# PSUM as one tile of eight banks, and row maxima and exponentials of two heads by one instruction each

## The chip, the core and the metric

The kernel runs on one core of a Trainium2 chip. The metric is device time in microseconds (us) of one execution. A core has TensorE (PE; its weight loads are listed as PEld), VectorE (DVE), ScalarE (ACT), GpSimd (POOL) and SyncE (SP, which here issues DMAs). Each engine works through its own instructions in program order and waits on semaphores for the others. PSUM, the memory that matmuls write, has eight banks of 512 fp32 values on each of 128 partitions.

## What is computed

The reference is a stack of four layers on x of shape 8 x 512 x 128 (batch, sequence, width). Each half layer is `x = x + layernorm(f(layernorm(x)))`.

```
x = x + ln(L0_attn(ln(x)));  x = x + ln(L0_ffn(ln(x)))     # softmax attention; RWKV channel mix
x = x + ln(L1_attn(ln(x)));  x = x + ln(L1_ffn(ln(x)))     # test-time training; switch experts
x = x + ln(L2_attn(ln(x)));  x = x + ln(L2_ffn(ln(x)))     # linear attention; expert-choice experts
x = x + ln(L3_attn(ln(x)));  x = x + ln(L3_ffn(ln(x)))     # softmax attention with rope; staggered experts
```

The change concerns the two softmax attentions, L0 and L3. Both have 16 heads of width 8:

```
scores = q @ k.T  (512 x 512 per batch and head, L3 divides by sqrt(8))
out    = softmax(scores, axis=-1) @ v
```

## The kernel before

The work is one program with no loops on the chip; Python loops write out every instruction, and the order in which they are written is the order on each engine. Four parts follow each other: L0 attention with the L0 feed-forward, the L1 learner and routing in its background; a middle part (rest of L1, all of L2); L3 attention with the L3 feed-forward in its background; and a short tail that ends the last feed-forward.

Both attentions use `Attention.run` (L380). A *call* n is one batch with four heads; there are 32 calls in each attention. A call is cut into NJ = 4 blocks of 128 rows, and a *step* g handles one block, so an attention has 128 steps, plus lead and end. A tile `qk` holds q and k of the four heads, each head on its own group of 32 partitions, so that matmuls of four heads occupy four row groups of TensorE. An fp32 matmul shows as two MATMUL records and two weight loads in the trace.

The softmax is made in two passes over the scores:

- `score(g, h)` (L387) makes the scores with queries on the partitions (matmul at L393 into a bank called `at_s`), and VectorE takes the negated row maximum (L394) into `at_mx`.
- `maxima(n, mx)` (L368) transposes the maxima of a whole call on TensorE (L372), copies them (L374) and sends them by four DMAs (L376) into a spare row of `qk`, so that the second product subtracts them.
- `weigh(g, h)` (L396) makes the scores again, transposed (matmul at L400 into a bank called `at_st`), and ScalarE takes the exponential (L403) into `at_e`.
- `total_up(n)` (L405) multiplies the exponentials of a call with v (L411, 32 MATMUL records in one bank, `at_o`) and copies the result (L419). `finish(n)` (L421) transposes it (L425) and divides by the sum that a column of ones gave (L428, L429).

`score` runs LEAD = 7 steps ahead of `weigh`. At each end of an attention, seven steps therefore have only one of the two. In a full step the order of the four score heads and the four exponential heads is s0, t2, s1, t3, then background work that costs little (`bg.between`), then s2, t0, s3, t1:

```
for i in (0, 2):
    for h in range(2):
        if is_s: score(ahead, i + h)
        if is_t: weigh(g, 2 - i + h)
    if i == 0 and (is_s or is_t): bg.between()
```

After that come, where they are due, `maxima`, `total_up` and `finish`, and then `bg.pull` (L296), which writes out pieces of background work. `Background` (L253) is a planner: every piece yields its estimated cost on TensorE and VectorE, and `pull` takes pieces until 5.0 us of TensorE or 3.0 us of VectorE (L0), or 3.3 and 2.5 us (L3), are used. In L3 these pieces are the projection of the next batch (L1766 and the VectorE and GpSimd work after it) and the feed-forward of finished batches (`hidden`, L1923 and L1924; `result`, L1930 and L1933). The costs do not depend on how long anything takes on the chip, so the order of the background is fixed by the program.

Every PSUM user takes a bank by `cx.bank(name)` (L118), which turns through RING = 8 tags:

```
self.turn[0] += 1
return self.ps.tile([P, 512], F32, name=name, tag=f"bank{self.turn[0] % self.RING}", bufs=1)
```

A tag has one buffer, so the ninth bank asked for waits until all users of the first have finished with it. Eight heads of a full step take eight banks; then the background's banks follow in the same ring.

Of the kernel before, what the change touches and what calls it, by code (L numbers as in the profile page):

```python
# [9 lines left out]
F32 = mybir.dt.float32  # L10
I32 = mybir.dt.int32
AF = mybir.ActivationFunctionType
ALU = mybir.AluOpType
AX = mybir.AxisListType
PSUM = bass.MemoryType.PSUM
DRAM = bass.MemoryType.DRAM

P = 128
# [3 lines left out]
NJ = S // P  # L22
# [48 lines left out]
class Ctx:  # L71


    def __init__(self, es: ExitStack, tc: tile.TileContext, consts: bass.AP):
        self.tc = tc
        nc = self.nc = tc.nc
        pool = lambda name, bufs, **kw: es.enter_context(tc.tile_pool(name=name, bufs=bufs, **kw))
        self.keep = pool("keep", 1)
        self.shared = pool("shared", 2)
        self.dram = pool("dram", 1, space=DRAM)  # L80

        self.c = self.keep.tile([P, C_ALL], F32, name="consts_sb", tag="consts_sb")
        nc.sync.dma_start(self.c, consts)
        self.ident = self.c[:, C_ID : C_ID + P]
        self.triu = self.c[:, C_TRIU : C_TRIU + P]
        self.ones = self.keep.tile([P, P], F32, name="ones", tag="ones")
        nc.vector.memset(self.ones, 1.0)
        self.mhalf = self.keep.tile([P, 8], F32, name="mhalf", tag="mhalf")
        nc.vector.memset(self.mhalf, -0.5)
        self.x = [self.keep.tile([P, NJ, D], F32, name=f"x{b}", tag=f"x{b}") for b in range(B)]  # L90

        self.home = self.keep

        self.ps = pool("ps", 1, space=PSUM)
        self.turn = [0]
        es.enter_context(tc.manual_schedule())

        self.brisk = False
# [17 lines left out]
            yield other  # L116

    def bank(self, name):  # L118
        self.turn[0] += 1
        return self.ps.tile([P, 512], F32, name=name, tag=f"bank{self.turn[0] % self.RING}", bufs=1)  # L120

    def work(self, shape, name, bufs=2, dtype=F32):
        return self.w.tile(shape, dtype, name=name, tag=name, bufs=bufs)
# [197 lines left out]
class Attention:  # L321
# [58 lines left out]
    def run(self, n_calls, load, dst, done, scale, bg):  # L380


        cx, nc = self.cx, self.cx.nc
        total = NJ * n_calls
        mx, es, ots = {}, {}, {}

        def score(g, h):  # L387
            n, c = divmod(g, NJ)
            qk = self.qks[n % self.NQK][32 * h : 32 * h + 32]
            if n not in mx:  # L390
                mx[n] = cx.work([P, NJ, 4], "at_mx", bufs=3)
            s = cx.bank("at_s")
            nc.tensor.matmul(s, qk[:, 0, c * P : (c + 1) * P], qk[:, 1, :], start=True, stop=True)  # L393
            nc.vector.tensor_reduce(mx[n][:, c, h : h + 1], s, AX.X, ALU.max, negate=True)  # L394

        def weigh(g, h):  # L396
            n, c = divmod(g, NJ)
            qk = self.qks[n % self.NQK][32 * h : 32 * h + 32]
            s = cx.bank("at_st")
            nc.tensor.matmul(s, qk[:, 1, c * P : (c + 1) * P], qk[:, 0, :], start=True, stop=True)  # L400
            if g not in es:
                es[g] = cx.work([P, 4, S], "at_e", bufs=5)
            nc.scalar.activation(es[g][:, h, :], s, AF.Exp, scale=scale)  # L403

        def total_up(n):  # L405
            o = cx.bank("at_o")
            vp = self.pads[n % self.NPAD]
            for c in range(NJ):
                e = es.pop(NJ * n + c)
                for h in range(4):  # L410
                    nc.tensor.matmul(  # L411
                        o[32 * h : 32 * h + 32, :],
                        vp[:, c, h, :],
                        e[:, h, :],
                        start=(c == 0),
                        stop=(c == NJ - 1),
                    )
            ots[n] = cx.work([P, S], "at_ot")
            nc.scalar.copy(ots[n], o)  # L419

        def finish(n):  # L421
            ot = ots.pop(n)
            t = cx.bank("at_ops")
            for c in range(NJ):
                nc.tensor.transpose(t[:, c * P : (c + 1) * P], ot[:, c * P : (c + 1) * P], cx.ident)  # L425
            t = t.rearrange("p (c h d) -> p c h d", c=NJ, h=4)
            rec = cx.work([P, NJ, 4, 1], "at_rec")
            nc.vector.reciprocal(rec, t[:, :, :, 8:9])  # L428
            nc.vector.tensor_mul(dst(n), t[:, :, :, 0:8], rec.to_broadcast([P, NJ, 4, 8]))  # L429
            done(n)  # L430

        for g in range(-self.LEAD - self.LOAD, total + 2):
            ahead = g + self.LEAD
            is_s, is_t = 0 <= ahead < total, 0 <= g < total
            n, c = divmod(ahead + self.LOAD, NJ)
            if c == 0 and 0 <= n < n_calls:
                self.fill(n, *load(n))
            for i in (0, 2):

                for h in range(2):  # L440
                    if is_s:
                        score(ahead, i + h)
                    if is_t:
                        weigh(g, 2 - i + h)
                if i == 0 and (is_s or is_t):
                    bg.between()
            spent = 0.0
            n, c = divmod(ahead - 4, NJ)
            if c == 0 and 0 <= n < n_calls:
                self.maxima(n, mx.pop(n))  # L450
            n, c = divmod(g - NJ, NJ)
            if c == 0 and 0 <= n < n_calls:
                total_up(n)
                spent += 3.6
            if c == 1 and 0 <= n < n_calls:
                finish(n)
                spent += 0.5
            if is_s or is_t:
                bg.pull(spent)
# [147 lines left out]
class Mix:  # L607
# [16 lines left out]
    def load(self):  # L624
        cx, nc = self.cx, self.cx.nc
        W_r, W_k, W_v, mu_r, mu_k = self.args
        self.mu = cx.const([D, 2], "mu")
        nc.sync.dma_start(self.mu[:, 0:1], mu_r.rearrange("(d o) -> d o", o=1))
        nc.sync.dma_start(self.mu[:, 1:2], mu_k.rearrange("(d o) -> d o", o=1))
        raws = []  # L630
        for i, w in enumerate((W_r, W_k, W_v)):
            raws.append(cx.work([P, D], f"l0f_raw{i}", bufs=1))
            nc.sync.dma_start(raws[-1], w)
        self.nu = cx.const([D, 2], "nu")
        yield
        yield
        yield
        nc.vector.tensor_scalar(self.nu, self.mu, -1.0, 1.0, ALU.mult, ALU.add)
        t = cx.bank("l0f_w_ps")
        for i in range(3):  # L640
            nc.tensor.transpose(t[:, i * P : (i + 1) * P], raws[i], cx.ident)
        w = cx.const([P, 3, P], "w0f")
        nc.scalar.copy(w[:, 0:2, :].rearrange("p i d -> p (i d)"), t[:, : 2 * P])

        nc.scalar.mul(w[:, 2, :], t[:, 2 * P : 3 * P], 0.5)
        self.wr, self.wk, self.wv = (w[:, i, :] for i in range(3))
        yield 0.4
# [1414 lines left out]
```

## Time and profile before

| | us |
|---|---|
| median of 3 runs | 2136.73 |
| lowest and highest run | 2125.67, 2138.96 |
| the profiled execution | 2132.52 |
| its span, first to last instruction | 2130.7 |
| PE busy in the span | 1772.0 |
| DVE busy | 1290.8 |
| ACT busy | 1085.9 |
| first and last score matmul, L0 attention (L393) | 40.6, 708.7 |
| first and last score matmul, L3 attention (L393) | 1339.4, 2018.2 |

The profile is one execution of the program. An engine's busy time is the union of its instructions' durations. "PE" counts matmuls, which overlap; their ends are modelled by the profiler's reader. A group line gives line, engine, operation, output <- inputs, shapes and count, then the busy time in us and the mean duration in ns, then the idle time of the engine just before these instructions and what ended it. A line of waits names who waited for whom, total us, times, and the longest. In the order of time, a line gives start, length, engine, line and operation; instructions of one kind that follow each other are merged (x2, x8).

### The profile page before, as it was taken

To read this page: it belongs to the slowest core of one execution; us is meant where nothing else is said; L and a number is where in the kernel's file an instruction comes from. 1 tells how busy PE (TensorE), PEld (TensorE's weight loads), DVE (VectorE), ACT (ScalarE), POOL (GpSimd) and SP (SyncE) were. 2 spreads that over 40 slices of the span, in tenths; PEclk is the share of its full clock that TensorE was granted. 3 is DMA by queue.
4 is the path that set the end of the run, shared out by engine and by line. 5 is a ranking of instruction groups with operands and counts; after the bars stand their busy time and mean duration, and the time that the engine had idled before them with its cause. 6 is when DMAs were issued, how large, how long until landed. Compare 5 with 4: busy or idle time off the path is not lost.

```text
span 2130.7 us, 31833 instructions
## 1 busy us (share of the span) xinstructions
PE 1772.0 (83%) x10886; PEld 1012.4 (48%) x10886; DVE 1290.8 (61%) x4012; ACT 1085.9 (51%) x2272; POOL 500.2 (23%) x566
## 2 busy tenths in 40 slices
PE   3999999898989967649446773799999999999996
PEld 1444545454534456437335552444554454545454
DVE  2777786777777665546447422777666666665522
ACT  1566655555554732346552221366666565665653
POOL 1001111112121122442523485222212121110001
PEclk7999988899988887659565786799999999999998
DMA  5212101011100032016214132111101010100000
GB/s 127 39 33 39 34 16 38 14 39 22 32 16 15 14 104 83 23 27 180 79 50 124 24 42 36 31 32 29 27 9 31 11 27 12 29 12 6 9 6 10
DMA packets 198064, 81.83 MB, mean 38 GB/s; under 512 B 97604, under 2 KB 189674, under 8 KB 197904
## 3 DMA queue, kind: packets, MB, share of 16 engines
q1 hardware_dynamic: 190224, 73.61, 14.3%
q0 software_dynamic: 7680, 6.19, 1.9%
q8 instruction: 87, 1.43, 0.3%
q14 instruction: 73, 0.60, 0.1%
HBM read 45.25 MB, written 31.59 MB: 36 GB/s over the span
## 4 chain that ended last, share of the span: by engine, by line
PE 55%; DVE 23%; ACT 6%; issue 6%; POOL 5%; DMA 3%; SPq 2%; POOLq 0%; ACTq 0%; DVEq 0%
PE at_o L411 11%; PE at_s L393 11%; DVE at_mx L394 8%; PE at_st L400 6%; PE l3f_y_ps L1930 5%; PE l3f_h_ps L1923 5%; DVE ln_st L203 2%; PE flip L239 2%; POOL l2f_out L1686 2%; POOL ln_rs L194 1%; PE l1f_h_ps L1155 1%; PE l1f_y_ps L1177 1%; POOL l2f_xg L1081 1%; PE at_ops L425 1%; DVE ln_mv L205 1%
## 5 line engine op out<-in xcount | busy, mean ns | idle before, releaser
L394 DVE TENSOR_REDUCE at_mx<-at_s 128x1 f32<-128x512 f32 x1024 | 642.3, 681 | 302.3 <-PE at_st L400 233.9
L393 PE MATMUL at_s<-qk 32*128 32x512 f32 x2048 | 612.0, 655 | 35.6 <-DMA qk<-qk_zero 21.3
L403 ACT ACTIVATE at_e<-at_st 128x512 f32<-128x512 f32 x1024 | 535.7, 597 | 193.6 <-PE at_st L400 152.4
L400 PE MATMUL at_st<-qk 32*128 32x512 f32 x2048 | 610.2, 655 | 18.4 <-DVE at_mx L394 12.6
L194 POOL TENSOR_TENSOR ln_rs<-ln_ve,mhalf 128x4 f32<-128x4 f32 x136 | 138.3, 1017 | 837.5 <-DVE ln_ve L188 773.7
L393 PEld LDWEIGHTS at_s<-qk 32*128 32x128 f32 x2048 | 232.2, 194 | 177.4 <-issue 57.7
L400 PEld LDWEIGHTS at_st<-qk 32*128 32x128 f32 x2048 | 240.5, 192 | 111.7 <-issue 41.8
L411 PE MATMUL at_o<-at_e,pad_v 128*32 128x512 f32 x2048 | 254.2, 641 | 14.8 <-DVE at_mx L394 14.8
L411 PEld LDWEIGHTS at_o<-at_e,pad_v 128*32 128x32 f32 x2048 | 66.9, 117 | 197.5 <-issue 173.8
L1930 PEld LDWEIGHTS l3f_y_ps<-w3f,l3f_hT 128*128 128x128 f32 x1024 | 131.8, 197 | 46.3 <-issue 26.8
L1930 PE MATMUL l3f_y_ps<-w3f,l3f_hT 128*128 128x128 f32 x1024 | 136.9, 282 | 3.2 <-ACT l3f_hT L1924 2.0
L419 ACT COPY at_ot<-at_o 128x512 f32<-128x512 f32 x64 | 37.5, 585 | 199.5 <-PE at_o L411 199.5
L1923 PE MATMUL l3f_h_ps<-l3f_xT,w3f 128*128 128x512 f32 x256 | 131.2, 611 | 0.0
L1924 ACT ACTIVATE l3f_hT<-l3f_h_ps,w3f_b1c 128x512 f32<-128x512 f32 x128 | 85.0, 683 | 64.1 <-PE l3f_h_ps L1923 64.0
L1933 DVE SCALAR_TENSOR_TENSOR l3f_o<-l3f_y_ps,l3f_w,l3f_o 128x128 f32<-128x128 f32 x128 | 44.4, 348 | 93.3 <-PE l3f_y_ps L1930 93.1
L217 ACT ACTIVATE l_xn<-x,ln_off,ln_rs 128x128 f32<-128x128 f32 x96 | 39.5, 482 | 81.5 <-DVE ln_off L211 75.4
L239 PE MATMUL flip<-consts_sb,l_xn 128*128 128x128 f32 x96 | 29.6, 398 | 54.4 <-ACT l_xn L217 54.1
L203 DVE BATCH_NORM_STATS2 ln_st<-x 128x6 f32<-128x128 f32 x256 | 55.2, 278 | 18.2 <-POOL x L937 12.4
L1686 POOL DMA_INDIRECT l2f_out<-l2f_y,l2f_idx x32 | 50.5, 1579 | 21.9 <-DVE l2f_y L1683 13.1
L1923 PEld LDWEIGHTS l3f_h_ps<-l3f_xT,w3f 128*128 128x128 f32 x256 | 42.2, 194 | 23.9 <-issue 10.0
L1773 POOL TENSOR_TENSOR l_qk<-l_r,consts_sb 128x256 f32<-128x256 f32 x32 | 21.9, 686 | 133.2 <-DVE l_r L1768 133.2
L366 POOL COPY pad_v<-l_in 128x128 f32<-128x128 f32 x32 | 9.4, 294 | 185.4 <-DMA l_in<-l_v 147.9
(412 smaller groups left out, 2551.0 us busy)
## 6 DMA issues: line engine op xcount, KB each, us to landing
l1f_w<-in_L_ffn_w SPq DMA_DIRECT2D x32, 256.0 KB
l2f_parts<-l2f_out SPq DMA_DIRECT2D x32, 256.0 KB
l2f_out<-l1f_zero SPq DMA_DIRECT2D x24, 256.0 KB
l_qk<-l_qkT SPq DMA_DIRECT2D x16, 256.0 KB
qk<-l_qk SPq DMA_DIRECT2D x128, 32.0 KB
qk<-at_mt SPq DMA_DIRECT2D x256, 2.0 KB
qk<-l_qkT SPq DMA_DIRECT2D x128, 32.0 KB
l2f_x<-l2f_rows SPq DMA_DIRECT2D x8, 272.0 KB
```

The lines of the kernel that those rows point to most:

```text
L194: self.nc.gpsimd.tensor_tensor(rs, ve, self.mhalf[:, :NJ], ALU.pow)
L203: nc.vector.bn_stats(st[:, j, :], src[:, j, :])
L239: self.nc.tensor.transpose(t[:, j * P : (j + 1) * P], src[:, j, :], self.ident)
L393: nc.tensor.matmul(s, qk[:, 0, c * P : (c + 1) * P], qk[:, 1, :], start=True, stop=True)
L394: nc.vector.tensor_reduce(mx[n][:, c, h : h + 1], s, AX.X, ALU.max, negate=True)
L400: nc.tensor.matmul(s, qk[:, 1, c * P : (c + 1) * P], qk[:, 0, :], start=True, stop=True)
L403: nc.scalar.activation(es[g][:, h, :], s, AF.Exp, scale=scale)
L411: nc.tensor.matmul(o[32 * h : 32 * h + 32, :], vp[:, c, h, :], e[:, h, :], start=(c == 0), stop=(c == NJ - 1),)
L1686: nc.gpsimd.indirect_dma_start(out=self.pairs.summed[s], out_offset=bass.IndirectOffsetOnAxis(ap=idx[e][:, s : s + 1], axis=0), in_=ys[e][ ...
L1923: nc.tensor.matmul(hp, self.w1[:, e, f * P : (f + 1) * P], xt, start=True, stop=True)
L1924: nc.scalar.activation(hts[e][:, f], hp, AF.Relu, bias=self.b1c[:, f, e : e + 1])
L1930: nc.tensor.matmul(yp[:, :D], hts[e][:, f, js], self.w2[:, e, f, :], start=(f == 0), stop=(f == NF - 1))
```

## The change

PSUM becomes one tile of eight banks, allocated once. `bank` returns a slice of one bank, and the new `twin` returns a slice of two neighbouring banks, starting at an even one; if the turn is odd, one bank is passed over. Waits between users of a bank now come from overlapping accesses to that tile, instead of from giving back a buffer.

`score` and `weigh` each handle two heads. Their matmuls move to `products`, which writes two heads into the two halves of a twin. One reduction then reads both banks (128 x 2 x 512) and writes two maxima per row, and one exponential reads both banks and writes two heads of `at_e`. In each half step, the two products for the exponentials are written first, then the two for the maxima, then the exponential, then the reduction. So the order of heads on TensorE is t2, t3, s0, s1, and after `bg.between` t0, t1, s2, s3. In a full step the banks go, in ring order, to a pair t, a pair s, a pair t and a pair s.

```
-        self.ps = pool("ps", 1, space=PSUM)
+        self.banks = pool("ps", 1, space=PSUM).tile([P, self.RING, 512], F32, name="banks", tag="banks")
...
     def bank(self, name):
+        k = self.turn[0]
         self.turn[0] += 1
-        return self.ps.tile([P, 512], F32, name=name, tag=f"bank{self.turn[0] % self.RING}", bufs=1)
+        return self.banks[:, k % self.RING, :]
+
+    def twin(self, name):
+
+        k = self.turn[0] + self.turn[0] % 2
+        self.turn[0] = k + 2
+        return self.banks[:, k % self.RING : k % self.RING + 2, :]
...
-        def score(g, h):
+        def products(s, g, i, side):
+
             n, c = divmod(g, NJ)
-            qk = self.qks[n % self.NQK][32 * h : 32 * h + 32]
+            for h in (i, i + 1):
+                qk = self.qks[n % self.NQK][32 * h : 32 * h + 32]
+                nc.tensor.matmul(
+                    s[:, h - i, :],
+                    qk[:, side, c * P : (c + 1) * P],
+                    qk[:, 1 - side, :],
+                    start=True,
+                    stop=True,
+                )
+
+        def score(g, i, s):
+            n, c = divmod(g, NJ)
             if n not in mx:
                 mx[n] = cx.work([P, NJ, 4], "at_mx", bufs=3)
-            s = cx.bank("at_s")
-            nc.tensor.matmul(s, qk[:, 0, c * P : (c + 1) * P], qk[:, 1, :], start=True, stop=True)
-            nc.vector.tensor_reduce(mx[n][:, c, h : h + 1], s, AX.X, ALU.max, negate=True)
-
-        def weigh(g, h):
-            n, c = divmod(g, NJ)
-            qk = self.qks[n % self.NQK][32 * h : 32 * h + 32]
-            s = cx.bank("at_st")
-            nc.tensor.matmul(s, qk[:, 1, c * P : (c + 1) * P], qk[:, 0, :], start=True, stop=True)
+            nc.vector.tensor_reduce(mx[n][:, c, i : i + 2], s, AX.X, ALU.max, negate=True)
+
+        def weigh(g, i, s):
             if g not in es:
                 es[g] = cx.work([P, 4, S], "at_e", bufs=5)
-            nc.scalar.activation(es[g][:, h, :], s, AF.Exp, scale=scale)
+            nc.scalar.activation(es[g][:, i : i + 2, :], s, AF.Exp, scale=scale)
...
-                for h in range(2):
-                    if is_s:
-                        score(ahead, i + h)
-                    if is_t:
-                        weigh(g, 2 - i + h)
+                if is_t:
+                    st = cx.twin("at_st")
+                    products(st, g, 2 - i, 1)
+                if is_s:
+                    s = cx.twin("at_s")
+                    products(s, ahead, i, 0)
+                if is_t:
+                    weigh(g, 2 - i, st)
+                if is_s:
+                    score(ahead, i, s)
```

## The prediction

> **What bounds the kernel now.** I read the page's totals first, then busy time by stage, then the chain of the work that ended last by stage, then the waits of TensorE's weight loads, and last one step of the loop in order of time. The stages in the second view are the first attention (45 to 735 us), the middle (735 to 1340), the last attention (1340 to 2052) and the tail.
>
> ```profile
> span 2130.7 us, 31833 instructions
> ...
> PE 1772.0 (83%) x10886; PEld 1012.4 (48%) x10886; DVE 1290.8 (61%) x4012; ACT 1085.9 (51%) x2272; POOL 500.2 (23%) x566
> ...
> PE 55%; DVE 23%; ACT 6%; issue 6%; POOL 5%; DMA 3%; SPq 2%; POOLq 0%; ACTq 0%; DVEq 0%
> ```
> ```profile
> 45.00:735.00 690.00, 634.17 (x4040) 311.86 (x4037) 509.95 (x1427) 398.17 (x845) 104.36 (x128) 0.91 0.14 28
> 735.00:1340.00 605.00, 387.39 (x1875) 298.38 (x1877) 292.45 (x1299) 224.01 (x501) 245.55 (x243) 0.71 0.27 69
> 1340.00:2052.00 712.00, 677.55 (x4590) 352.19 (x4587) 465.57 (x1188) 431.96 (x871) 132.92 (x162) 0.98 0.09 20
> ```
>
> The columns after the stage's length are PE, PEld, DVE, ACT and POOL busy, then TensorE's granted clock. In the last attention PE is busy 677.55 of 712 us (95%), VectorE only 465.57 (65%), ScalarE 431.96 (61%). In the first attention PE is busy 634.17 of 690 (92%), VectorE 509.95 (74%), ScalarE 398.17 (58%). So neither of the two engines whose instructions are merged is full. The chain by stage agrees: in the last attention PE has 74% of it and VectorE 19%; in the first, 59% and 29%, with "DVE at_mx L394" alone at 13.5% and 11.6%. The middle has no attention and the change leaves it alone.
>
> How do the reductions come onto the chain when VectorE is a third idle? Through the ring of banks. The weight loads' waits in the last attention (us in total, times, longest) say who waits:
>
> ```profile
> PEld at_mx_ps L372 <- DVE at_mx L394: 29.0, 31, 2.1
> ...
> PEld at_o L411 <- DVE at_mx L394: 19.3, 23, 1.7
> ...
> PEld l3f_y_ps L1930 <- DVE at_mx L394: 12.9, 26, 1.2
> ...
> PEld l_qkv_ps L1766 <- DVE at_mx L394: 10.3, 13, 1.2
> ```
>
> None of these reads anything that the latest reductions wrote (`maxima`, L370, wants reductions of an earlier step). They want a bank. A step with both kinds of scores takes eight banks, the whole ring, so the first background matmul after it gets the bank of the step's first score, and must wait for that score's reduction. One such step:
>
> ```profile
> 1503.84 1.29 DVE L394 TENSOR_REDUCE at_mx<-at_s 128x1 f32<-128x512 f32 x2 [0.34 <-PE at_st L400]
> 1503.94 1.08 ACT L403 ACTIVATE at_e<-at_st 128x512 f32<-128x512 f32 x2 [1.36 <-PE at_st L400]
> 1504.07 0.59 PE L400 MATMUL at_st<-qk 32*128 32x512 f32 x1
> 1504.08 0.60 PE L393 MATMUL at_s<-qk 32*128 32x512 f32 x2
> 1504.09 0.59 PE L400 MATMUL at_st<-qk 32*128 32x512 f32 x1
> 1504.61 0.16 PEld L411 LDWEIGHTS at_o<-at_e,pad_v 128*32 128x32 f32 x8 [0.76 <-DVE at_mx L394]
> ```
>
> The reader is to see a coincidence. Rounds of four matmuls on four row groups follow each other every 0.43 us (1503.22, 1503.65, 1504.08), so the last round has streamed by 1504.51. The first reduction ends at 1503.84 + 0.68 = 1504.52, and L411 starts 0.09 us later. Streaming and the bank's release end together: nothing is lost, and there is no slack either.
>
> **The change, part by part.** (1) *Merged reductions.* 1024 reductions become 512 of two rows of 512.
>
> ```profile
> L394 DVE TENSOR_REDUCE at_mx<-at_s 128x1 f32<-128x512 f32 x1024 | 642.3, 681 | 302.3 <-PE at_st L400 233.9 <-PE at_s L393 67.2
> L1322 DVE TENSOR_REDUCE l2a_n<-l2a_sq 128x32 f32<-128x256 f32 x32 | 11.2, 412 | 12.2 <-ACT l2a_sq L1317 12.2
> ```
>
> From 256 to 512 elements the duration grows by 681 - 412 = 269 ns, 1.05 ns per element, and L1322 has 32 rows in one instruction, so rows cost nothing visible. A merged one takes 681 + 512 x 1.05 = 1.22 us. Two back to back now take 0.60 (start to start, median of neighbours in the trace) + 0.68 = 1.28. Saved: 0.06 per pair, 512 x 0.06 = 32 us of VectorE. The Trainium skill, "Perfetto Trace Analysis", section "Optimizing Scalar/DVE Operations", puts the per-instruction access overhead of VectorE on PSUM at about 125 ns, which would make it an estimated 512 x 0.125 = 64 us; the row says half, because start to start already shows most of the fixed part hidden. I take the row. The same section says that grouping improves throughput "if the engine is saturated", and that if these engines are not saturated but cause bubbles on other engines, "breaking up instructions may allow work to be completed sooner". That is the rule against this change: at 65 to 74% busy its condition for grouping is not met, and the reductions' bubbles on PE are the waits above. With 125 ns the gain of (5) would be 176 x 0.125/1.28 = 17 us and the sum +27; by the second half, nothing is gained where PE waits, and (3) is the price.
>
> (2) *Merged exponentials.* Two now take 0.48 + 0.60 = 1.08 us (1503.94 above).
>
> ```profile
> L403 ACT ACTIVATE at_e<-at_st 128x512 f32<-128x512 f32 x1024 | 535.7, 597 | 193.6 <-PE at_st L400 152.4 <-PE at_s L393 39.2
> L1338 ACT ACTIVATE l2a_qkv<-l2a_qkv 128x1024 f32<-128x1024 f32 x8 | 8.3, 1041 | 0.0
> ```
>
> L643 (256 elements, 372 ns) and L419 (512, 585 ns) give 0.83 ns per element, so 597 + 426 = 1.02 us; the nearest row of that length is 1.04. I take 1.02: 0.06 per pair, 31 us of ScalarE, off the chain (ScalarE has 4% of it in both stages).
>
> (3) *The bank's release.* This is the part that decides. The twin for exponentials is now taken first, so the first background matmul after a full step gets a bank of the first exponential pair and waits for the whole merged instruction: 1503.94 + 1.02 + 0.08 (release to start, as at 1504.52 to 1504.61) = 1505.04 instead of 1504.61, 0.43 later. I looked at all 121 such steps of each stage in the trace and replaced the start of the first background matmul by the later of "streaming over + 0.09" and "first exponential's start + 1.10". Last attention: 113 steps have background work; in 66 it started both right after the first reduction and within 0.16 us of the end of streaming, and it moves by +0.43 each (28.4 us); 9 others move by 1.5 us in all; in 13 the reduction was late because VectorE was on other work, and it moves forward, -3.0 us. Together +26.9. PE idles only 34 us of 712 here, so most of it passes to the end; its share lies between PE's part of the chain, 0.74, and 1. I take 0.85: **+23 us**. First attention: 36 + 9 steps move by +32.7 us, 18 with a late reduction by -16.4. With PE at 59% of the chain the first counts +19; of the second I count half, -8, since where VectorE is late the third bank or the next twin waits for it anyway. **+11 us**.
>
> (4) *The turn between PE and VectorE.* Score matmuls that wait for a reduction's bank: 76 weight loads in the first attention, 29 in the last ("PEld at_s L393 <- DVE at_mx L394: 35.7, 76, 2.6" and "12.1, 29, 1.5"). Today the first head restarts while the second is still reduced. With twins both banks come free together at the end of the pair (0.06 sooner than the second), both products are made, and then 1.22 us is reduced where 0.68 was left: 1.22 - 0.68 - 0.06 = 0.48 longer per turn. At VectorE's chain shares: 76 x 0.48 x 0.29 + 29 x 0.48 x 0.19 = **+13 us**. Bounds: 0 (these waits lie beside others) and 105 x 0.48 = 50.
>
> (5) *Shorter reductions on the chain.* 13.5% of 690 plus 11.6% of 712 is 176 us; times 0.06/1.28 gives **-8 us**. The lead and end of each stage, seven steps with only one kind of score, are bound by that engine: 28 pairs x 0.06 for reductions and the same for exponentials, **-3 us**.
>
> (6) *At nothing.* The matmuls are the same, still four row groups in turn, each head in a bank of its own; the rounds overlap as now unless the two pairs are released apart (a rival). The bank skipped to even out a twin costs a slot in steps with an odd number of background banks; the next score's release by the background reader is as now. Single-bank users elsewhere keep their order. Pairs are already ready together: in 97% of cases the second reduction of a pair starts within 0.65 us of the first, so waiting for both products costs nothing. No DMA or SP or POOL work moves; `maxima` (L374 to L376) issues its four DMAs behind the same L372, up to 0.43 later, four steps before anyone needs them. Behind the waiting matmul on PE stands all the rest of the step; late next are the background's readers and then the next step's scores.
>
> Sum: 23 + 11 + 13 - 8 - 3 = +36 us. The profiled execution took 2132.52 (span 2130.7 and 1.8 around it), so 2168.5; the median of the runs is 4.2 above it, so **2173 us** is forecast.
>
> **Rivals.** *Absorbed* (0.27): the new wait stands where PE would have waited a little later anyway, and (3) and (4) pass on by 40% of what I take: 19 - 11 = +8, 2145 us. For it: 45% of the first attention's chain is not PE. Against it: PE at 95% in the last. *Faster* (0.13): exponentials go first and are no longer held up by a late reduction, so the score rounds are split less. Counting first starts within 0.2 us, the first attention has 716 rounds where 512 would do. A round is 0.43 us of PE, 0.25 at PE's share of the chain. The break-even is 36/0.25 = 144 of the 204 excess rounds; if all go and the -16.4 of late steps counts in full: 36 - 51 - 8 = -23, 2113 us. Against it: many splits come from waits that remain. *More splits* (0.10): pairs released apart turn a round of four into two of two, also in the last attention, where 412 of 618 rounds have all four. If 70 of its 256 half steps split, 70 x 0.86 x 0.85 = +51 on top, 2224 us. *One tile, one wait* (0.03): if the waits were kept for the whole tile and not by bank, PE would stand still during reductions, 256 steps x some 2.4 us = 2750 us; this would be the change not doing what it says.
>
> **How the numbers follow.** The likeliest case has 0.47, with 2150 to 2198 as its own range ((3) at PE's share or in full, (4) at 0 or double). Leaving out the whole-tile case, half of "more splits" and two thirds of "faster" (0.17 in all) gives 2118 to 2215. One per cent, about what a measurement of this kernel can tell from no change, is 21 us: slower by more than that needs over 2158. Likeliest beyond that line 0.44, with more splits and one tile 0.57; within it 0.30; faster 0.13.
>
> **What the profile after would show.** Merged reductions at about 1220 ns and exponentials at 1020. The first background loads after a step (L372, L411, L1766, L1923, L1930) waiting for the exponential instead of the reduction, 0.4 us longer in the last attention, where the stage should grow by some 20 us. "Single" rounds gone. The middle as long as before. I would be wrong if the last attention is not longer, if weight loads still name the reduction first, or if rounds of four are clearly more frequent in the first attention.

## The result, and the profile after

| | before | after |
|---|---|---|
| median of runs on the same chip, us | 2136.03 | 2165.2 (2161.47 to 2168.76) |
| ratio, 95% interval | 1 | 1.0145 [1.0107, 1.0183] |
| profiled execution, us | 2132.52 | 2164.64 |
| L0 attention and the middle, us | 1297.8 | 1306.4 |
| L3 attention, us | 712.5 | 736.1 |
| rounds of score matmuls in L0; in L3 | 716; 618 | 629; 595 |

The kernel became 1.45% slower, some 31 us. The forecast was 2173 us. A stage here runs from its first score matmul to the first of the next stage, and the L3 attention ends with its last exponential. Before the change its first score matmul is at 1338.4 us; the 1339.4 in the table of the kernel before is 1.0 too late. L0 and the middle are taken together, because the border between them moves by some microseconds from one profile to the next. Of the 32.1 us by which the two profiled executions differ, the L3 attention has 23.6 and all that lies ahead of it 8.6.

The page of the changed kernel, totals and the two merged groups (busy time, mean ns of one, idle time before them and what ended it):

```profile
span 2162.7 us, 31192 instructions
...
PE 1744.0 (81%) x10886; PEld 976.6 (45%) x10886; DVE 1259.5 (58%) x3500; ACT 1060.4 (49%) x1760; POOL 501.2 (23%) x566
...
L411 DVE TENSOR_REDUCE at_mx<-banks 128x2 f32<-128x1024 f32 x512 | 611.4, 1218 | 354.0 <-PE banks L399 351.5
...
L416 ACT ACTIVATE at_e<-banks 128x1024 f32<-128x1024 f32 x512 | 504.7, 1019 | 227.2 <-PE banks L399 217.1
```

VectorE does 31.3 us less and ScalarE 25.5 us less, and the end comes later. The reader is to see that the saving and the loss are on different engines. Busy time by stage of the changed kernel (length, PE, PEld, DVE, ACT, POOL, then the granted clock) shows where PE stands still:

```profile
45.00:744.70 699.70, 613.45 (x4100) 294.60 (x4096) 499.51 (x1196) 391.50 (x606) 106.15 (x130) 0.91 0.14 28
744.70:1346.90 602.20, 382.18 (x1811) 294.34 (x1811) 287.81 (x1275) 215.82 (x484) 244.62 (x240) 0.70 0.27 69
1346.90:2083.00 736.10, 673.59 (x4584) 337.33 (x4585) 448.94 (x931) 420.65 (x615) 133.00 (x162) 0.98 0.09 19
```

The last attention of the kernel before, by the same bounds:

```profile
1338.40:2050.90 712.50, 678.05 (x4586) 352.91 (x4586) 465.23 (x1187) 431.37 (x871) 132.92 (x162) 0.97 0.09 20
```

In the last attention PE is busy for 673.59 us, 4.5 less than before (678.05 in the same stage), but idle for 62.5 instead of 34.5. The clock is the same within 0.01 (0.97 before), so it is idle time and not slower matmuls. The waits of TensorE's weight loads in this stage say for whom:

```profile
PEld banks L379 <- ACT at_e L416: 32.4, 29, 2.1
PEld banks L424 <- ACT at_e L416: 27.1, 26, 1.5
PEld banks L1941 <- ACT at_e L416: 19.9, 18, 1.5
...
PEld banks L1784 <- ACT at_e L416: 14.4, 13, 1.5
...
PEld banks L1948 <- ACT at_e L416: 6.8, 6, 1.1
```

These are the transposed maxima (L379), the product with v (L424), `hidden` (L1941), the projection (L1784) and `result` (L1948). The prediction showed four of them under their old line numbers (L372, L411, L1766, L1930); the fifth, `hidden`, stood lower in the list of before:

```profile
PEld l3f_h_ps L1923 <- DVE at_mx L394: 7.3, 13, 0.8
```

Before, the five waited 78.8 us in total for the reduction "at_mx"; now it is 100.6 us for the exponential "at_e". One such step of the changed kernel, in order of time:

```profile
1515.95 1.04 PE L399 MATMUL banks<-qk 32*128 32x512 f32 x8
1516.23 1.94 ACT L416 ACTIVATE at_e<-banks 128x1024 f32<-128x1024 f32 x2 [1.33 <-PE banks L399]
1516.23 2.36 DVE L411 TENSOR_REDUCE at_mx<-banks 128x2 f32<-128x1024 f32 x2 [0.78 <-PE banks L399]
...
1517.30 0.59 PE L1784 MATMUL banks<-w3a,xnT 128*128 128x384 f32 x1 [0.31 <-ACT at_e L416]
```

The first merged exponential runs from 1516.23 for 1.02 us, to 1517.25; the projection's matmul, which reads nothing of it, starts at 1517.30, when it has let go of its two banks. The last matmul's modelled end is 1516.99, so even by that cautious end PE lost 0.31 us. Over the full steps of the stage that have background work, the median time from the end of streaming (start of the step's last score matmul plus 0.43) to the first background matmul, called the gap here, is 0.459 us after, 0.088 before; the sum of these gaps is 59.5 and 29.8 us.

### The profile page after: what moved, and what is told of

Its sections match the earlier page's. It is cut to its first block, busy times and chain, and to the rows that moved or that the text cites. A ratio compares the mean times of both kernels' runs of the same rounds, so it can differ in the third digit from the quotient of the medians.

```text
span 2162.7 us, 31192 instructions
## 1 busy us (share of the span) xinstructions
PE 1744.0 (81%) x10886; PEld 976.6 (45%) x10886; DVE 1259.5 (58%) x3500; ACT 1060.4 (49%) x1760; POOL 501.2 (23%) x566
## 4 chain that ended last, share of the span: by engine, by line
PE 30%; DVE 9%; ACT 8%; issue 5%; POOL 4%; DMA 2%; SPq 0%; POOLq 0%; ACTq 0%; DVEq 0%
PE banks L399 7%; PE banks L424 5%; PE banks L1948 5%; PE banks L1941 4%; ACT at_e L416 4%; DVE at_mx L411 3%; PE banks L246 2%; POOL l2f_out L1704 2%; DVE ln_st L210 1%; POOL ln_rs L201 1%; POOL l2f_xg L1099 1%; PE banks L1784 1%; PE banks L1489 1%; ACT ln_out L224 1%; DMA l_o<-l1f_given,l1f_place 1%
## 5 line engine op out<-in xcount | busy, mean ns | idle before, releaser
L411 DVE TENSOR_REDUCE at_mx<-banks 128x2 f32<-128x1024 f32 x512 | 611.4, 1218 | 354.0 <-PE banks L399 351.5
L399 PE MATMUL banks<-qk 32*128 32x512 f32 x4096 | 632.8, 667 | 70.0 <-ACT at_e L416 26.8
L416 ACT ACTIVATE at_e<-banks 128x1024 f32<-128x1024 f32 x512 | 504.7, 1019 | 227.2 <-PE banks L399 217.1
L399 PEld LDWEIGHTS banks<-qk 32*128 32x128 f32 x4096 | 254.9, 197 | 310.0 <-issue 117.6
L201 POOL TENSOR_TENSOR ln_rs<-ln_ve,mhalf 128x4 f32<-128x4 f32 x136 | 138.5, 1019 | 864.3 <-DVE ln_ve L195 801.3
L424 PE MATMUL banks<-at_e,pad_v 128*32 128x512 f32 x2048 | 239.8, 609 | 10.9 <-ACT at_e L416 10.3
L1948 PEld LDWEIGHTS banks<-w3f,l3f_hT 128*128 128x128 f32 x1024 | 129.6, 193 | 45.3 <-issue 34.5
L424 PEld LDWEIGHTS banks<-at_e,pad_v 128*32 128x32 f32 x2048 | 63.4, 112 | 185.8 <-issue 153.9
L1941 PE MATMUL banks<-l3f_xT,w3f 128*128 128x512 f32 x256 | 132.3, 612 | 8.2 <-ACT at_e L416 8.2
L1948 PE MATMUL banks<-w3f,l3f_hT 128*128 128x128 f32 x1024 | 133.9, 278 | 3.2 <-ACT at_e L416 1.8
L1942 ACT ACTIVATE l3f_hT<-banks,w3f_b1c 128x512 f32<-128x512 f32 x128 | 85.7, 683 | 72.0 <-PE banks L1941 61.4
L1941 PEld LDWEIGHTS banks<-l3f_xT,w3f 128*128 128x128 f32 x256 | 41.7, 194 | 34.8 <-ACT at_e L416 19.9
```

The costliest lines, as they stand in the source:

```text
L201: self.nc.gpsimd.tensor_tensor(rs, ve, self.mhalf[:, :NJ], ALU.pow)
L399: nc.tensor.matmul(s[:, h - i, :], qk[:, side, c * P : (c + 1) * P], qk[:, 1 - side, :], start=True, stop=True,)
L411: nc.vector.tensor_reduce(mx[n][:, c, i : i + 2], s, AX.X, ALU.max, negate=True)
L416: nc.scalar.activation(es[g][:, i : i + 2, :], s, AF.Exp, scale=scale)
L424: nc.tensor.matmul(o[32 * h : 32 * h + 32, :], vp[:, c, h, :], e[:, h, :], start=(c == 0), stop=(c == NJ - 1),)
L1941: nc.tensor.matmul(hp, self.w1[:, e, f * P : (f + 1) * P], xt, start=True, stop=True)
```

## The experiments

All are edits of the changed kernel unless said otherwise. Lengths and gap sums are from one profile each, which can lie some microseconds from its kernel's median ("order alone" has the shortest of its 22 runs); an empty cell was not worked out. The verdict rests on the ratios, each against the kernel before on the same chip.

| kernel | ratio [95%] | L0 and middle | L3 attention | L3 gap sum |
|---|---|---|---|---|
| before | 1 | 1297.8 | 712.5 | 29.8 |
| tile alone | 1.0016 [0.9999, 1.0033] | 1299.5 | 711.8 | 31.1 |
| skip alone | 1.0022 [1.0012, 1.0032] | 1300 | 713.5 | |
| order alone | 1.0026 [1.0014, 1.0037] | 1292 | 716.4 | |
| order and skip, all single | 1.0047 [1.0030, 1.0064] | 1309.7 | 718.8 | 27.1 |
| only reductions merged | 1.0047 [1.0023, 1.0071] | 1303.7 | 719.5 | 25.6 |
| first pair's exponential single | 1.0065 [1.0045, 1.0085] | 1301.8 | 718.8 | 26.4 |
| the change | 1.0145 [1.0107, 1.0183] | 1306.4 | 736.1 | 59.5 |
| only first pair's exponential merged | 1.0138 [1.0123, 1.0154] | 1299 | 732.4 | 56.6 |
| only exponentials merged | 1.0239 [1.0208, 1.0270] | 1319.5 | 739.8 | 59.1 |
| maxima first | 1.0301 [1.0279, 1.0323] | 1328.3 | 744.9 | 81.0 |
| wrap-only skip | 1.0782 [1.0767, 1.0797] | 1379.6 | 793.5 | |
| old order, wrap-only skip | 1.0390 [1.0375, 1.0406] | 1339 | 756.9 | |
| old order, even pairs | 0.9999 [0.9983, 1.0016] | 1289.3 | 716.2 | 25.7 |

**Nothing merged: the new order and the skipped bank alone.**

```
-            nc.vector.tensor_reduce(mx[n][:, c, i : i + 2], s, AX.X, ALU.max, negate=True)
+            for h in range(2):
+                nc.vector.tensor_reduce(mx[n][:, c, i + h : i + h + 1], s[:, h, :], AX.X, ALU.max, negate=True)
...
-            nc.scalar.activation(es[g][:, i : i + 2, :], s, AF.Exp, scale=scale)
+            for h in range(2):
+                nc.scalar.activation(es[g][:, i + h, :], s[:, h, :], AF.Exp, scale=scale)
```

> One tile, twins and the changed order of products are kept; each head has its own reduction and its own exponential again. Bank theory (the first background matmul after a full step waits for the whole merged exponential): with single exponentials its bank comes free after 0.60 us instead of 1.02, so the last attention (first score matmul to last exponential) goes back from 736.1 to about 712 us and the whole to about 2140 us. Rival, order or tile (the products' new order, the skipped bank or the waits of one tile cost the time): the last attention stays near 736 and the whole near 2165 us.

Measured: 2144.44 us beside 2133.25, 1.0047 [1.0030, 1.0064]; its profiled execution, 2150.93, was the longest of its six. Its page shows instructions of the old durations:

```profile
L412 DVE TENSOR_REDUCE at_mx<-banks 128x1 f32<-128x512 f32 x1024 | 643.3, 682 | 323.3 <-PE banks L399 322.3
...
L418 ACT ACTIVATE at_e<-banks 128x512 f32<-128x512 f32 x1024 | 535.1, 597 | 196.3 <-PE banks L399 194.5
```

So a third of the loss, some 10 us, is there with no instruction merged, and with the median gap still at 0.088. The last attention has 6.3 us of it in the one profile, and did not go back to 712. The prediction had put this part at nothing.

**Only the reductions merged.** The exponentials' edit above, without the reductions'.

> Reductions merged, exponentials single; twins and order as in the change. Bank theory: the first background bank is one of the exponentials' pair and comes free after 0.60 us, so the last attention is about 712 us or a little less and the whole about 2135 us. Turn theory (a merged reduction gives its banks back together and makes each turn between PE and VectorE 0.48 us longer, 13 us in all): about 13 us slower than with everything single.

Measured: 2141.49 us, 1.0047 [1.0023, 1.0071], the same ratio as with nothing merged. Merging 1024 reductions into 512 costs nothing that can be told here, and brings nothing either; the 13 us of the "turn theory" did not come.

**Only the exponentials merged.** The reductions' edit above, without the exponentials'.

> Exponentials merged, reductions single. Bank theory: the last attention stays at about 736 us and the whole at about 2160 to 2165 us, since the merged exponential alone makes the wait. Turn theory: the first attention gains up to 10 us and the whole is near 2155 us. If the merged reduction were the cause, the last attention would go back to about 712 us.

Measured: 2181.24 us, 1.0239 [1.0208, 1.0270]. Merged exponentials, on top of order and skip, cost 0.0192, 41 us; the merged reductions of the full change then win 20 us of it back. The expectation missed by 16 us, though not for the last attention (739.8 us where 736 was expected): most of what the full change wins back, 13.1 us in one profile each, lies ahead of it.

**Maxima first.** If the first background matmul pays for the instruction that frees the ring's oldest bank, then the pair that gets the oldest banks decides what it pays.

```
-                if is_t:
-                    st = cx.twin("at_st")
-                    products(st, g, 2 - i, 1)
                 if is_s:
                     s = cx.twin("at_s")
                     products(s, ahead, i, 0)
                 if is_t:
-                    weigh(g, 2 - i, st)
+                    st = cx.twin("at_st")
+                    products(st, g, 2 - i, 1)
                 if is_s:
                     score(ahead, i, s)
+                if is_t:
+                    weigh(g, 2 - i, st)
```

> Everything merged, but in each half step the pair for the maxima takes its twin, its products and its reduction first, then the pair for the exponentials. The first background bank is now one that a merged reduction (1.22 us) reads. Bank theory: its release is 0.1 to 0.2 us later than with a merged exponential (1.02 us, but starting up to 0.1 us after the reduction), in some 70 to 110 steps: the last attention is 5 to 20 us longer than 736, the first attention longer too since the wait is again for the busier VectorE; the whole 2175 to 2195 us. Rival, order (exponentials' products first is what costs): the last attention goes back toward 712 us.

Measured: 2195.29 us, 1.0301 [1.0279, 1.0323]. The background's weight loads in its last attention now wait for the reduction, but for 0.2 us:

```profile
PEld banks L379 <- DVE at_mx L411: 45.3, 31, 2.1
PEld banks L424 <- DVE at_mx L411: 29.2, 23, 2.2
...
PEld banks L1784 <- DVE at_mx L411: 16.6, 13, 1.4
```

The 1.22 us instruction now stands where the 1.02 us one stood. The median gap goes from 0.459 to 0.682 us, by 0.22, which is the difference of the two durations (0.20) and little more. The gap sum rises by 21.5 us and the stage by 8.8; another 21.9 us lie ahead of the stage.

**The tile alone**, on the kernel before: the tile of eight banks, and `bank` returning a slice of it; nothing else.

> The kernel before with PSUM as one tile of eight banks, nothing else: one bank per head, the order s0, t2, s1, t3 as before. With everything single but twins and the new order the whole took 1.0047 of before, and the middle part, which has no twins, some 7 us more than before. If the waits derived from one tile cost that: this run is at about 1.004 and its middle (last exponential of the first attention to the first score matmul of the last) at about 601 us instead of 593. If the twins' skipped banks or the new order cost it: 1.000 and 593 us.

Measured: 2135.25 us beside 2133.46, 1.0016 [0.9999, 1.0033]; 13 runs. The one tile keeps its waits by bank: it can't be told from no change, and 0.33% is the most that it may cost. But its middle took 602.5 us, as in the change, and not the 593 of before, while its first attention (first score matmul to last exponential) took 697.0 instead of 704.3. So the border between the two moved with the tile alone, and the longer middle is not a cost of the merging.

**The first pair's exponential single.** If only the hold on the oldest two banks costs time, then it is enough to keep that one exponential of the step in two parts. The other one of each step, and all reductions, stay merged.

```
-            nc.scalar.activation(es[g][:, i : i + 2, :], s, AF.Exp, scale=scale)
+            if i == 2:
+                for h in range(2):
+                    nc.scalar.activation(es[g][:, i + h, :], s[:, h, :], AF.Exp, scale=scale)
+            else:
+                nc.scalar.activation(es[g][:, i : i + 2, :], s, AF.Exp, scale=scale)
```

> The changed kernel, but the exponentials of the first half step alone (the pair whose banks the first background matmul gets) are two instructions again; three quarters of the merging stays. Bank theory: the wait falls from 1.02 to 0.60 us, and the whole is at 2138 to 2145 us, as with all exponentials single (2141.5). If the merged exponentials cost by something other than that bank (longer turns at any pair, ScalarE's other work kept waiting), about half of the 24 us between the two stays: near 2153 us.

Measured: 2144.37 us, 1.0065 [1.0045, 1.0085]. Out of the 31 us, 17 are gone with this edit alone. A step of it in order of time, before its product with v:

```profile
1513.05 1.09 ACT L418 ACTIVATE at_e<-banks 128x512 f32<-128x512 f32 x2 [1.25 <-PE banks L399]
1513.15 2.35 DVE L411 TENSOR_REDUCE at_mx<-banks 128x2 f32<-128x1024 f32 x2 [0.46 <-PE banks L399]
1513.82 0.16 PEld L428 LDWEIGHTS banks<-at_e,pad_v 128*32 128x32 f32 x8 [0.76 <-ACT at_e L418]
```

The first of the two exponentials (0.60 us) ends at 1513.65 and the weight load starts at 1513.82; the second has the next bank until 1514.14. The median gap is 0.088 again, as before the change. In the last attention PE is idle 42.4 us instead of the 62.5 of the full change, and the stage is 718.8 us long instead of 736.1.

**The order alone.** The kernel with nothing merged, with two single banks instead of a twin, so that no bank is skipped:

```
-                    st = cx.twin("at_st")
+                    st = [cx.bank("at_st"), cx.bank("at_st")]
...
-                    s = cx.twin("at_s")
+                    s = [cx.bank("at_s"), cx.bank("at_s")]
```

> One tile, the new order t, t, s, s, everything single, and no bank passed over to make a pair start at an even bank (single banks one after the other). If the skipped banks cost the 10 us that single instructions left (2144.4 against 2133.3): about 2134 us. If the order or the tile does: about 2144 us.

Measured: 2136.28 us, 1.0026 [1.0014, 1.0037].

**The skip alone**, on the kernel with the tile alone, in the old order of heads:

```
             for i in (0, 2):
+                if is_s or is_t:
+                    cx.turn[0] += cx.turn[0] % 2
```

> One tile, single banks and the old order s, t, s, t, but the ring is moved on to an even bank ahead of each half step, as twins do. If the skipped banks cost the 10 us: about 2144 us. If the new order does: as the run with the tile alone.

Measured: 2136.41 us, 1.0022 [1.0012, 1.0032]. Order and skip each cost at most some 8 us with the tile's share in it, and about 10 together; their intervals touch that of the tile alone, so the runs do not divide the 10 us any finer.

**The old order with merged reductions.** Exponentials single, the products written s0, t2, s1, t3 again, and a bank skipped only where a pair would run over the end of the ring:

```
-        k = self.turn[0] + self.turn[0] % 2
+        k = self.turn[0] + (self.turn[0] % self.RING == self.RING - 1)
...
-                    products(st, g, 2 - i, 1)
                 if is_s:
                     s = cx.twin("at_s")
-                    products(s, ahead, i, 0)
+                for h in range(2):
+                    if is_s:
+                        product(s, ahead, i, 0, h)
+                    if is_t:
+                        product(st, g, 2 - i, 1, h)
```

> Reductions merged, exponentials single, banks given as t, t, s, s, but the products written in the old order s0, t2, s1, t3, and a bank passed over only where a pair would run over the end of the ring. Bank theory with a small cost of order and skips (each 0.1 to 0.25%): what the merged reductions save (3 us against everything single) is left without those costs, so 2128 to 2136 us, level with before or just below. Turn theory (merged reductions cost about 13 us): 2145 us or more.

Measured: 2213.62 us beside 2130.53, 1.0390 [1.0375, 1.0406]: 83 us where little was expected. The expectation was wrong. The next but one and the last run tell why.

**Only the first pair's exponential merged**, everything else single: the opposite of the run above that left it single.

> Everything single (as e1, 2144.4 us) except the exponentials of the first half step, whose banks the first background matmul gets: a quarter of the merging and the whole of the wait. Bank theory: some 15 to 25 us slower than e1, 2160 to 2170 us, with the last attention near 736. If the cost grew with the number of merged exponentials: a quarter to a half of the 37 us between e1 and e3, about 2150 to 2160 us.

Measured: 2158.02 us, 1.0138 [1.0123, 1.0154]. Against the kernel with nothing merged it is 0.0091, 19 us, from 128 exponentials per attention; the median gap is 0.470. The same cost was 17 us when taken away from the full change.

**The changed kernel with the wrap-only skip.** One line, the first of the edit above.

> The changed kernel, but a bank is passed over only where a pair would run over the end of the ring, not wherever the turn is odd. If skipped banks are a cost of their own beside the wait: 3 to 6 us less than the changed kernel, about 2160 us. If they are nothing: 2165 us.

Measured: 2297.26 us, 1.0782 [1.0767, 1.0797], by the ratios (0.0637 of 2131) 136 us more than the change. The expectation missed this too. A step of its last attention:

```profile
1618.53 1.94 ACT L416 ACTIVATE at_e<-banks 128x1024 f32<-128x1024 f32 x2 [0.41 <-PE banks L399]
1618.69 1.23 DVE L411 TENSOR_REDUCE at_mx<-banks 128x2 f32<-128x1024 f32 x1 [0.68 <-PE banks L399]
...
1619.61 0.18 PEld L399 LDWEIGHTS banks<-qk 32*128 32x128 f32 x1 [1.11 <-ACT at_e L416]
...
1619.61 0.69 PE L399 MATMUL banks<-qk 32*128 32x512 f32 x1 [0.28 <-ACT at_e L416]
```

Here it is a score matmul (L399) of the step that waits 1.11 us for an exponential of the same step. A step that starts at an odd bank takes 1-2, 3-4 and 5-6; bank 7 can't hold a pair, so the last pair goes to 0-1, and bank 1 is still held by the step's first exponential. With pairs on even banks four pairs always fit the eight banks. Over the whole span these waits of score matmuls for exponentials grow from 57.6 us in 60 of the change to this:

```profile
PEld banks L399 <- ACT at_e L416: 152.3, 143, 3.6
```

The loss does not show as idle time of PE. The last attention by the same columns as above:

```profile
1419.80:2213.35 793.55, 732.49 (x4585) 359.05 (x4586) 453.75 (x931) 422.40 (x615) 132.56 (x162) 0.96 0.08 18
```

PE is idle 61.1 us there, against 62.5 in the change, but busy 58.9 us longer for the same matmuls, and the score matmuls go in 699 rounds instead of 595, of which 328 instead of 428 have all four row groups. So the waits split rounds, and fewer matmuls overlap. The granted clock is lower too (0.96 and 0.98 here; over the whole span 0.851 and 0.871 in the median of the runs); what share of the 136 us it has was not tried. The split rounds are a case of what the "more splits" rival described.

**The old order with even pairs.** The old-order kernel with the skip as the change has it; only that line differs.

> As e9 (reductions merged, exponentials single, banks t, t, s, s, products in the old order s0, t2, s1, t3), but pairs start at an even bank again, so that a full step takes exactly eight banks. Bank theory: the 80 us that e9 lost came from the step's last pair meeting the banks of its own first pair; with even pairs they go, and 1.000 to 1.004 of before is left (2130 to 2140 us). If the old order of products with merged reductions was the cause in e9: 1.03 or more.

Measured: 2129.09 us beside 2129.74, 0.9999 [0.9983, 1.0016]. So the 83 us were the odd starts and nothing else. In the last attention they go with rounds again: 656 with odd starts, 571 with even ones, and no more idle PE (39.3 and 46.3 us). This kernel has merged reductions and single exponentials, like "only reductions merged", and differs from it in the order of the heads alone: 1.0047 against 0.9999, so that the order t2, t3, s0, s1 costs some 10 us where the reductions are merged. But the granted clock differs too. Its mean over the span is 0.867 in the median of the runs of "only reductions merged", and 0.8745 here. Among the 50 runs of the kernel before that stand beside the tile alone, a straight line gives 1.7 us more for each 0.001 of clock less (clocks from 0.867 to 0.877), which would make an estimated 13 us of the difference. So the 10 us may come by way of the clock; whether the order lowers it was not tried. The first pair's exponential is not open to this doubt: in both of its comparisons the slower kernel had the higher clock (0.871 against 0.866, 0.8745 against 0.869).

The old order with even pairs is the best merged version tried, and level with the kernel before, which no kernel of these beats beyond its interval.

## Why the prediction was right, and where its steps were not

The total was right: +36 us forecast from 2132.52 of the profiled execution, +32.1 found in the profiled executions and 0.0145, 31 us, in the runs. The bound was read rightly: PE idle time in the last attention, not the work of VectorE or ScalarE, sets the end. But terms of the sum had the wrong size, and one was put at nothing. Forecast were 34 for the bank's release, 13 and -8 for the reductions, -3 for lead and end and 0 for order and skip; the runs give 17 for the release, 4 for the second pair's exponential, nothing that can be told for the reductions, and 10 for order and skip. That the sums lie within 5 us of each other is in part luck. So is the last attention: it grew by 23.6 us where some 20 were forecast, but 6.3 of these are there with nothing merged.

*(1) and (2), durations.* 1.22 and 1.02 us were forecast; 1218 and 1019 ns came. Saved were 31.3 us of VectorE (32 forecast) and 25.5 of ScalarE (31). The rule of the Trainium skill that the prediction weighed ("Perfetto Trace Analysis", "Optimizing Scalar/DVE Operations") came out as the row had it: 0.60 + 0.68 - 1.22 = 0.06 us saved by a merged reduction, not 0.125. Its warning on engines that are not saturated but cause bubbles elsewhere is what the first-pair runs show, at 17 to 19 us.

*(3), the bank's release: +34 forecast (23 and 11), +17 found.* The mechanism stands. The waits changed their name from "at_mx" to "at_e", the typical gap grew by 0.37 us (0.43 forecast), the first pair's exponential alone takes 17 us away and 19 us back, and a longer instruction in its place (maxima first) costs more. The gaps in the last attention are 33 us longer in sum than with that exponential single, somewhat more than the +26.9 of the forecast. What was too large is the share passed on. I took 0.85; from 26.4 to 59.5 us of gap the stage grew by 17.3, a share of 0.52, and from 59.5 to 81.0 by 8.8, a share of 0.41, in one profile each. Only a part of the 33 us was absorbed by waits elsewhere: PE's idle time grew by 26 us inside the gaps and fell by 6 us in the rest of the stage, 20 in all. The other 7 us are a matter of counting, since a gap starts with the end of streaming and idle time only with the modelled end of the last matmul, 0.16 us later. So the "absorbed" rival was near in size for this term (it kept 40% of what I took; 17 of 34 came), but its mechanism is seen for only 6 of the 33 us. PE's share of the chain (0.74) did not measure the share passed on. Ahead of the last attention, where 11 us were forecast, the two profiles differ by 4.6.

*(4) and (5), the turn between PE and VectorE and the shorter reductions: +13 and -8 forecast, nothing found.* Merging the reductions changed nothing where the exponentials are single (1.0047 and 1.0047) and won 20 us where they are merged (1.0239 to 1.0145). Together they were to cost 5 us. Beside single exponentials that can't be told from nothing (the two intervals together leave some 6 us either way), beside merged ones it is refuted; no run separates (4) from (5). Why the merged reductions win 20 us beside merged exponentials, and none beside single ones, stays open; 13.1 of it lie ahead of the last attention.

*(6), put at nothing: +10 found.* The order of the heads and the skipped bank, with nothing merged, cost 0.0047 [0.0030, 0.0064]. The order by itself costs some 10 us where the reductions are merged (1.0047 against 0.9999); with everything single the difference is 0.0010 without the skip and 0.0025 with it, each near the noise of the two kernels compared. The tile has no measurable share in it. Two things go with the new order: more rounds of score matmuls in the last attention (633 against 612 with everything single and no skip, 640 against 601 with the skip, 609 against 571 with merged reductions), so that rounds of four are split; and a lower granted clock where the reductions are merged. Which of them costs the time is not shown. For the order by itself, then, the prediction's reason for nothing, that the rounds overlap as now, did not hold.

*The rivals.* "Faster" needed 144 of the 204 excess rounds of the first attention to go. 87 went (716 to 629), and the first attention did not get shorter: so a round there is worth less than the 0.25 us that I gave it, or its gain was lost to the longer gaps (56.2 us in sum instead of 30.2). One of the signs of being wrong that the prediction named did come: rounds of four in the first attention rose from 333 to 393. It did not bring what it was to be a sign of, a faster first attention: that stage took 704.3 us before and 704.2 after. "More splits" is refuted for the change: rounds in the last attention fell from 618 to 595, and those with all four rose from 412 to 428. "One tile, one wait" is refuted by the tile alone.

In one sum, stepwise by the runs: order and skip +10, merged reductions 0, second pair's exponential +4 (its interval includes nothing), first pair's exponential +17, together +31. The steps do not simply add up in another sequence: with single reductions, the second pair's exponential costs 1.0239 - 1.0138, 22 us instead of 4. This goes with what is left open under (4).

The middle was forecast as long as before, and took 593 us before and 602 after, in one profile each. With the tile alone, at no cost that can be told in the whole, it took 602.5 as well, with a first attention 7.3 us shorter than before: the border moved, and the merging is not the reason. Why it moves with the tile was not traced.

## What to carry to other kernels

When two reads of PSUM become one, ask first who wants the banks next: the merged instruction keeps both until its end, and its first bank comes free one whole half later. Replay the trace with the later release to find the gaps, expect only a part of what they add at the end (here 0.41 to 0.52), and measure by splitting that one instruction again. Where groups of banks share a ring with single ones, let the groups start at multiples of their size: here that one line was worth 83 and 136 us, and the count of rounds showed it where PE's idle time did not.

## What the runs showed of the hardware

- One VectorE or ScalarE instruction reads across two banks at no extra price: 681 to 1218 ns is 1.05 ns per added element, and 597 to 1019 ns is 0.82, the prices that the prediction took from instructions of 256 and 512 elements (1.05, with an SBUF tile as the shorter one, and 0.83).
- Two neighbouring slices of one PSUM tile are waited for separately: with the tile alone the ratio is 1.0016 [0.9999, 1.0033], and in the step of the first-pair run PE starts while the second exponential still reads the next bank.
- 28 us more of PE idle time (34.5 to 62.5 in the last attention) made that stage only 23.6 us longer, since PE's busy time fell by 4.5 for the same matmuls. With fewer rounds (618 to 595) more of them overlap, which would shrink the union of their durations; that this is the cause was not tried. The wrap-only skip went the other way: 699 rounds, and PE busy 58.9 us longer than in the change. PE busy time alone is no measure of matmul work here.
- The same kernel ran at mean granted clocks from 0.867 to 0.877 (50 runs of the kernel before, beside the tile alone, 2139 to 2123 us), with some 1.7 us more for each 0.001 less: kernels that differ by 10 us can't be compared without looking at the clock.
